# Layer 1 of a two-layer graph attention kernel: gathers without a limit of five in flight, issued by half block

## The chip, the cores and the metric

The kernel runs on one core of a Trainium2 chip. The core has a matrix engine (TensorE, "PE" in the profile; its weight loads are "PEld"), a vector engine (VectorE, "DVE"), a scalar engine (ScalarE, "ACT"), a general engine (GpSimd, "POOL") and a queue engine (SyncE, "SP"), which work side by side and wait for each other on semaphores, and 16 DMA engines that move data between memory and the on-chip SBUF. The metric is the device time of one execution in microseconds. The kernel before has a median of 1829.56 us over three runs (1821.65 to 1831.82).

## The reference

Two graph attention layers over 2708 nodes with 1024 features, in float32. `adj` is a 2708 x 2708 matrix of zeros and ones, symmetric, with ones on the diagonal and about 16 others in a row.

```python
def layer0(x):                       # all products 1024 wide
    f, g = x @ Wf + bf, x @ Wg + bg
    e = relu(f @ g.T)
    attention = softmax(where(adj > 0, e, -9e15), axis=1)
    return attention @ (x @ W + bW)

def layer1(x):
    h = x @ W1
    e = leaky_relu(h @ a1 + (h @ a2).T, 0.2)
    attention = softmax(where(adj > 0, e, -9e15), axis=1)
    return relu(attention @ h)

x = layernorm(x + layer0(x))
x = layernorm(x + layer1(x))
```

## The kernel before

Since a row of `adj` has few ones, the kernel does not compute the 2708 x 2708 scores. A first stage reads `adj`, extracts the neighbours of every node as a list of up to 40, orders the nodes by the length of their lists, and cuts them into 85 groups of 32 nodes. A group whose longest list has up to 4n entries has n *tiles*: `TILES[g]` is 3 to 10. A tile has 128 partitions, four neighbours of each of 32 nodes, and is filled by one *gather*: an indirect DMA issued by POOL (line 180) that fetches 128 rows of a table in memory by the indices in one column of `SL`. Padding in the lists has an index past the table, and such a row is skipped. Four groups form a *block* (the first block is one group alone); there are 22 blocks and 405 tiles.

Layer 0 (lines 855 to 1090) works through the blocks with gathers of `x` into a ring of 20 slots. Its normalised output goes in two places: rows of x1 to the table `X1S`, and rows of x1 with the product by W1 a2 as a further column to the table `T1` (1028 columns, 4112 bytes a row).

Layer 1 (lines 1093 to 1247) is where the change lies. Its ring has 33 slots: the 20 of `ring` and 13 of `more`. Blocks go in order of their number of tiles, and each is cut into two *half blocks* of two groups, 43 in all, with 6 to 14 tiles each (the very first has 3). For half block n, in the order of the program:

- `sums` (line 804): on PE, for each tile four matmuls of its 128 x 512 halves by the weights in `st`, into one of two PSUM halves `po`; afterwards the tiles' slots are put in the set `free`;
- `closing` (line 1203): the scatter of an earlier block's finished rows to `out`, on POOL;
- `lay.gathers()` (line 1206): POOL's gathers for all tiles whose slot (their number less 33) is in `free`;
- a piece of an earlier block's product with W1: 16 matmuls into `pm`, and the transposes `pt` of the half block before;
- `scores1` for half block n + 1 (line 1122): on DVE the scores, the softmax's maximum and the weights `st`, with the exponential on ACT. This reads the last column of each gathered slot, so it waits for the gathers to land; the sums of n + 1 then wait for it;
- `out` on ACT: the sums scaled into `y`;
- `close1` (line 1142): SP loads the block's rows of `X1S` into one of three buffers `rb`, `u1b`, `u2b`; DVE adds them to the product and normalises; the scatter to `out` follows one half block later.

Every engine's instructions are kept in program order (class `InOrder`, line 61). A gather into a used slot must wait for the last reader of that slot: the scores on DVE and the last matmul on PE. The framework also gives each DMA that POOL issues one of eight semaphores in turn, and a DMA waits until the previous one on its semaphore has landed, unless another wait covers that. On top of that, `Halves(..., 5)` at line 1106 sets `flight` to 5: each gather from the sixth on waits for the landing of the fifth gather before it (lines 666 to 672). Layer 0's `Layer` has no `flight`.

Because `lay.gathers()` goes through the slots in order of their number, and each slot has its own last matmul, every gather of a half block carries its own wait for PE. The tiles of a half block are numbered by tile position and then group (line 635), which is also the order in which `sums` reads them.

Of the kernel before, what the change touches and what calls it, by code (L numbers as in the profile page):

```python
# [57 lines left out]
TILES = [SORTED[_g] for _g in GROUPS]  # L58
# [48 lines left out]
def listed_path(ctx, tc, x, adj, Wf, bf, Wg, bg, W, bW, W1, a1, a2, out):  # L107
# [6 lines left out]
    TW = D + 4  # L114
# [18 lines left out]
    pe, dve, act, pool, sp = (InOrder(tc, e) for e in (nc.tensor, nc.vector, nc.scalar, nc.gpsimd, nc.sync))  # L133
# [9 lines left out]
    T1 = dram.tile([N, TW], F32, name="T1")  # L143
# [20 lines left out]
    SL = const.tile([P, NG, QT], I32, name="SL")  # L164
    SL0 = const.tile([P, NSL0, QT], I32, name="SL0")
# [12 lines left out]
        nc.gpsimd.memset(t, 0.0)  # L178

    def gather(engine, dst, table, idx, rows=N):  # L180
        return engine.indirect_dma_start(
            out=dst, out_offset=None, in_=table,
            in_offset=bass.IndirectOffsetOnAxis(ap=idx, axis=0), bounds_check=rows - 1, oob_is_err=False)

# [9 lines left out]
    with tc.tile_pool(name="pre", bufs=1) as pre:  # L194
# [294 lines left out]
        for b in range(NB):  # L489
            n = nsize[b]  # L490
# [15 lines left out]
        t = pre.tile([P, NB], F32, name="badt")  # L506
        nc.vector.scalar_tensor_tensor(t, tot, 1.0, cnt, op0=ALU.mult, op1=ALU.not_equal, accum_out=bad[:, 1:2])
        t = pre.tile([P, NB], F32, name="badu")
        nc.vector.tensor_scalar(t, cnt, 0.0, 0.0, op0=ALU.is_equal, op1=ALU.add, accum_out=bad[:, 2:3])
        t = pre.tile([P, NB], F32, name="badv")  # L510
# [131 lines left out]
    class Layer:  # L642

        def __init__(self, units, rings, width, table, stp, flight=None):
            self.flight, self.issued = flight, []
            self.units, self.table, self.width, self.stp = units, table, width, stp

            self.first = {g: i for i, g in enumerate(g for u in units for g in u.gs)}  # L650
            self.slots = [(t, i) for t in rings for i in range(t.shape[1])]
            self.count = len(self.slots)
            self.order = [(u, g, t) for u in units for _, g, t in u.tiles]
            assert all(self.first[g] < NSL0 for _, g, _ in self.order[:self.count])
            self.next, self.free, self.most = 0, set(), len(self.order)
# [2 lines left out]
            t, k = self.slots[m % self.count]  # L658
            return t[:, k, :self.width]

        def gathers(self):
            while self.next < min(self.most, len(self.order)) and (self.next < self.count or self.next - self.count in self.free):
                u, g, t = self.order[self.next]
                idx = SL[:, g, t:t + 1] if self.next >= self.count else SL0[:, self.first[g], t:t + 1]
                made = gather(pool, self.rows(self.next), self.table, idx)
                if self.flight is not None:
                    if len(self.issued) >= self.flight:
                        tc.add_manual_dep(
                            made.ins, self.issued[-self.flight],
                            mybir.DependencyInfo(mybir.DependencyClass.Sync, mybir.DependencyReason.DATA),  # L670
                            reason="gathers in flight")
                    self.issued.append(made.ins.name)
                self.next += 1

        def soft(self, u):

            sc, shape = u.sc, [P, u.G, u.T]
            mq = small.tile([P, Q], F32, name="mq")
            dve.tensor_reduce(mq[:, :u.G], sc, AX.X, ALU.max)

            m4 = small.tile([32, Q, Q], F32, name="m4")
            for q in range(Q):
                dve.tensor_copy(m4[:, :u.G, q], mq[32 * q:32 * q + 32, :u.G])
            m1 = small.tile([32, Q], F32, name="m1")
            dve.tensor_reduce(m1[:, :u.G], m4[:, :u.G, :], AX.X, ALU.max)
            for q in range(Q):
                dve.tensor_copy(mq[32 * q:32 * q + 32, :u.G], m1[:, :u.G])
            dve.tensor_tensor(sc, sc, mq[:, :u.G].unsqueeze(2).to_broadcast(shape), op=ALU.subtract)
            act.activation(sc, sc, AF.Exp)
            u.st = self.stp.tile([P, MOST, 32], F32, name="st")  # L690
            k = 0
            while k < u.G:

                n, t = 1, TILES[u.gs[k]]
                while k + n < u.G and TILES[u.gs[k + n]] == t:
                    n += 1
                c, some = u.col[k, 0], [P, n, t, 32]
                dve.tensor_tensor(u.st[:, c:c + n * t, :].rearrange("p (g t) i -> p g t i", g=n),
                                  sc[:, k:k + n, :t].unsqueeze(3).to_broadcast(some),
                                  stack.unsqueeze(1).unsqueeze(1).to_broadcast(some), op=ALU.mult)  # L700
                k += n
            u.rs = small.tile([P, Q], F32, name="rs")
            dve.tensor_reduce(u.rs[:, :u.G], sc, AX.X, ALU.add)
# [57 lines left out]
    class Halves(Layer):  # L761
# [42 lines left out]
        def sums(self, u, po, ks):  # L804

            st, at, col = u.st[ks[0]], 0, {}
            for k in ks:
                col[k] = at
                at += TILES[u.gs[k]]
            index = {(k, t): m for m, (k, g, t) in enumerate(u.tiles)}  # L810
            for t in range(max(TILES[u.gs[k]] for k in ks)):
                for k in ks:
                    n = TILES[u.gs[k]]
                    if t < n:
                        for h in range(H):
                            j = place(k, h)
                            pe.matmul(po[j:j + 32], st[:, col[k] + t, :],
                                      self.rows(u.at + index[k, t])[:, h * 512:(h + 1) * 512],
                                      start=(t == 0), stop=(t == n - 1))
            self.free.update(u.at + m for (k, t), m in index.items() if k in ks)  # L820

        def spans(self, ks):

            return [slice(0, P)] if len(ks) == 2 else [slice(place(ks[0], h), place(ks[0], h) + 32) for h in range(H)]
# [19 lines left out]
    def load_lists(b):  # L844
        for g in groups[b]:
            gather(pool, SL[:, g, :], LD[:, :], idq[:, g:g + 1], N * Q)
# [8 lines left out]
    ring = ctx.enter_context(tc.tile_pool(name="ring", bufs=1)).tile([P, R0, TW], F32, name="ring")  # L855
    with ExitStack() as s0s:
# [3 lines left out]
        stp, xp, yp, jp = (new_pool(n, 1) for n in ("stp0", "xp", "yp", "jp0"))  # L860
        zs = new_pool("zp", 1).tile([P, TW], F32, name="z")
        seq = [1, 0, *range(2, NB)]
        units = cut(R0, 2, seq)
        lay = Layer(units, [ring], D, x, stp)
# [147 lines left out]
        for k, u in enumerate(units):  # L1012
# [6 lines left out]
            po = ps_s.tile([P, H, 512], F32, name="po")  # L1019
# [73 lines left out]
    with ExitStack() as s1s:  # L1093
# [3 lines left out]
        stp = new_pool("stp1", 3)  # L1097

        x1 = [rb, u1b, u2b]
        more = new_pool("ring1", 1).tile([P, R1 - R0, TW], F32, name="more")  # L1100

        order1 = sorted(range(NB), key=lambda b: (sum(TILES[g] for g in groups[b]), b))
        units = cut(R1, 2, order1)
        for u in units:
            u.st, u.ri = {}, {}
        lay = Halves(units, [ring, more], TW, T1[:, :], stp, 5)
        done1 = {b: i for i, b in enumerate(order1)}
        for u in units:
            g, at = u.gs[0], lay.first[u.gs[0]]
# [82 lines left out]
        def turn_half(u, ks, y):  # L1192
            b = u.b
            if ks[0] == 0:
                yT[b] = tp.tile([P, KC, P], F32, name="yT")
            steps = lay.turn(y, ks, yT[b])
            next(steps)
            return steps

        for n, (u, ks) in enumerate(parts):  # L1200
            b, po = u.b, banks[:, n % 2, :]
            lay.sums(u, po, ks)
            for _ in closing:
                pass
            closing = iter(())
            lay.gathers()
            made = pieces.pop(0)() if pieces else None
            steps = iter(())
            if turning is not None:
                v, kv, _ = turning  # L1210
                steps = turn_half(*turning)
                if kv[-1] + 1 == v.G:
                    pm = []
                    pieces += [lambda c=v.b, h=h, pm=pm: piece(c, h, pm) for h in range(H)]
            if n + 1 < len(parts):
                scores1(*parts[n + 1])
            y = yp.tile([P, 512], F32, name="y1")
            lay.out(u, po, ks, y)
            for _ in steps:
                pass  # L1220
            turning = u, ks, y
            if ks[-1] + 1 == u.G:
                k = done1[b]
                for i in (2 * k, 2 * k + 1):
                    if i < NB:
                        mark_over(i)
                if k == NB // 2 + 1:
                    count_over()
                if k + 2 == NB:
                    unfit = nc.values_load(flag[0:1, 0:1])  # L1230
            if made is not None:
                closing = close1(*made)
                next(closing)
        while pieces:
            made = pieces.pop(0)()
# [375 lines left out]
```

## Time and profile before

| | |
|---|---|
| median of 3 runs | 1829.56 us (1821.65 to 1831.82) |
| the profiled execution | 1827.94 us, its span 1826.2 us |
| PE busy | 1605.9 us (88%) |
| DVE busy | 1294.1 us (71%) |
| POOL busy | 1184.2 us (65%) |
| ACT busy | 642.9 us (35%) |
| layer 1's gathers | 405 issues, first at 1158.3 us, last at 1767.6 us, about 0.99 us of POOL each |
| sums of layer 1 on PE | 1170 to 1782 us; PE busy 526.75 us in 612.20 |
| POOL's DMA queue, whole span | 132032 packets, 428.29 MB |

The span runs from the first to the last instruction. The page divides it into 40 slices of 45.65 us and gives for each the busy tenths of every engine, the granted PE clock, the mean busy share of the 16 DMA engines and the rate in GB/s. POOL's busy time for a gather is the time to write its descriptors; the data lands later, and the trace gives the time from issue to landing. A wait for several semaphores is put down by the profile to the one that came last by its own reckoning, which can name an engine that had long been done.

### The profile page before, as it was taken

The page shows a single profiled execution, that of the slowest core. Times are in us where ns is not written, and L with a number is a line of the kernel's source. Part 1 is how long each engine was busy: PE and PEld are TensorE (multiplying, and loading weights), DVE is VectorE, ACT ScalarE, POOL GpSimd, SP SyncE. Part 2 cuts the span into 40 slices and gives each one's busy share as a digit, 9 for nine tenths or more (in the row PEclk, how much of TensorE's full clock was granted, in tenths as well). Part 3 has the DMA queues.
Part 4 walks back from the last instruction along what each step waited for, and adds up shares of the span by engine and source line. Part 5 has one row for each costly group of instructions (what it writes and reads, how often), then busy time and mean ns, then how long its engine had stood idle before and what let it go on. Part 6 is the DMA issues. An engine that isn't in the chain of part 4 may idle for free. (4 is left out here: it accounts for less than half of the span.)

```text
span 1826.2 us, 23203 instructions
## 1 busy us (share of the span) xinstructions
PE 1605.9 (88%) x6969; PEld 675.9 (37%) x6969; DVE 1294.1 (71%) x4262; ACT 642.9 (35%) x902; POOL 1184.2 (65%) x1192
## 2 busy tenths in 40 slices
PE   5999489899999999999999999298889798978896
PEld 3444233344444444444444444033333333333332
DVE  5779757888888888888888877365555446545552
ACT  4545344445555555444445552011111111111111
POOL 7888475676666666666666552576777676666650
PEclk8999799999999999999999999699899988989888
DMA  7646167667777777777766774799999999999970
GB/s 276 246 151 234 40 232 303 250 218 260 266 282 284 284 272 280 288 291 283 286 249 237 280 300 178 268 365 321 339 354 364 337 353 330 350 356 350 356 265 37
DMA packets 149987, 502.81 MB, mean 275 GB/s; under 512 B 32340, under 2 KB 32372, under 8 KB 147144
## 3 DMA queue, kind: packets, MB, share of 16 engines
q0 software_dynamic: 132032, 428.29, 64.9%
q1 hardware_dynamic: 10202, 55.72, 8.1%
q10 hardware_dynamic: 7618, 17.23, 2.5%
q8 instruction: 57, 0.93, 0.2%
q14 instruction: 78, 0.64, 0.1%
HBM read 509.64 MB, written 33.75 MB: 298 GB/s over the span
## 5 line engine op out<-in xcount | busy, mean ns | idle before, releaser
L71 POOL DMA_INDIRECT ring<-in_x_dram,SL x405 | 437.1, 1079 | 252.8 <-issue 91.1
L71 DVE SCALAR_TENSOR_TENSOR j<-ring,Fr 128x1024 bf16<-128x1024 f32 x402 | 494.5, 1230 | 81.7 <-DMA ring<-in_x_dram,SL 54.2
L71 PE MATMUL po<-ring,st 128*32 128x512 f32 x2616 | 334.2, 635 | 57.3 <-ACT y L71 40.3
L71 ACT COPY Fr<-pm 32x1024 f32<-32x1024 f32 (+2 forms) x353 | 340.5, 964 | 19.4 <-PE pm L71 14.7
L71 POOL DMA_INDIRECT ring<-T,SL x249 | 246.9, 992 | 114.2 <-issue 43.4
L71 PE MATMUL pm<-M,yT 128*128 128x512 f32 (+1 forms) x704 | 313.3, 598 | 0.5 <-ACT yT L71 0.5
L71 PE MATMUL pm<-M,xT 128*128 128x512 f32 x672 | 304.6, 607 | 0.0
L71 PE MATMUL pm<-Wt,xT 128*128 128x512 f32 (+1 forms) x704 | 303.5, 599 | 1.0 <-DMA Wt<-in_L_gnn_W_dram 1.0
L71 ACT ACTIVATE scores<-scores 128x12 f32<-128x12 f32 (+9 forms) x65 | 14.0, 216 | 726.7 <-DVE scores L71 726.7
L71 POOL DMA_INDIRECT more<-T,SL x156 | 154.6, 991 | 71.3 <-issue 32.8
L71 PEld LDWEIGHTS pm<-M,yT 128*128 128x128 f32 (+1 forms) x704 | 127.9, 186 | 184.6 <-issue 183.1
L71 PEld LDWEIGHTS po<-ring,st 128*32 128x32 f32 x2616 | 103.4, 117 | 243.6 <-issue 192.3
L71 PEld LDWEIGHTS pm<-M,xT 128*128 128x128 f32 x672 | 126.2, 193 | 162.2 <-issue 162.2
L71 PEld LDWEIGHTS pm<-Wt,xT 128*128 128x128 f32 (+1 forms) x704 | 125.1, 186 | 152.8 <-issue 151.0
L409 POOL TENSOR_TENSOR adj<-adj,iota 128x2708 f32<-128x2708 f32 (+3 forms) x23 | 130.5, 5684 | 23.9 <-ACT adj L71 23.8
L71 PE MATMUL po<-more,st 128*32 128x512 f32 x624 | 96.5, 714 | 38.1 <-ACT y L71 38.1
L412 DVE MAX8 cand<-adj 128x8 f32<-128x136 f32 (+2 forms) x440 | 97.3, 285 | 38.3 <-POOL adj L409 38.3
L71 PE MATMUL pm<-halfT,WfT 128*128 128x512 f32 x256 | 114.5, 603 | 1.1 <-ACT WfT L71 1.1
L71 DVE TENSOR_SCALAR scores<-ring,f1q 128x4 f32<-128x4 f32 (+6 forms) x69 | 17.4, 263 | 131.8 <-DMA ring<-T,SL 122.5
L71 POOL DMA_INDIRECT SL<-LD,idq x85 | 85.9, 1011 | 25.8 <-issue 21.2
L71 DVE TENSOR_SCALAR scores<-more,f1q 128x3 f32<-128x3 f32 (+6 forms) x48 | 12.5, 268 | 82.6 <-DMA more<-T,SL 73.7
L71 PEld LDWEIGHTS pm<-halfT,WfT 128*128 128x128 f32 x256 | 48.4, 193 | 58.1 <-issue 55.4
(211 smaller groups left out, 1547.8 us busy)
## 6 DMA issues: line engine op xcount, KB each, us to landing
adj<-in_adj_dram SPq DMA_DIRECT2D x21, 1354.0 KB, 5.9
X1S<-z SPq DMA_DIRECT2D x19, 512.0 KB, 6.5
ring<-in_x_dram,SL POOLq DMA_INDIRECT x405, 6.3
rows<-in_L_gnn_Wg_dram ACTq DMA_DIRECT2D x8, 512.0 KB, 4.4
rows<-in_L_gnn_Wf_dram ACTq DMA_DIRECT2D x8, 512.0 KB, 3.6
rows<-in_L_gnn_W_dram ACTq DMA_DIRECT2D x8, 512.0 KB, 6.3
Wt<-in_L_gnn_W_dram ACTq DMA_DIRECT2D x1, 4096.0 KB
M<-in_L_gnn_W_dram SPq DMA_DIRECT2D x1, 4096.0 KB
```

The source lines that it names most:

```text
L71: made = self.tc.keep_in_program_order(op(*args, **kwargs))
L409: nc.gpsimd.tensor_tensor(k[:n, cut], k[:n, cut], iota[:n, cut], op=ALU.mult)
L412: nc.vector.max(cand[:n, s, :], k[:n, s * SEG:min((s + 1) * SEG, N)])
```

## The change

The argument 5 and the code of the limit are removed. `sums` now returns the number of the tile that it reads last (the last tile of the half block's longest group), and `gathers` first collects all tiles whose slot is free and, if the tile that goes into that last-read slot is among them, issues it ahead of the others. Since that gather waits for the last matmul of the half block, the gathers behind it in POOL's order find their own matmuls done and carry no wait for PE. PE, DVE, ACT and SP have the same instructions in the same order in both kernels; on POOL the same number of gathers, with one of them moved to the front of nearly every batch. In the compiled program each of POOL's DMAs in layer 1 now waits for the eighth of POOL's DMAs before it, through the eight semaphores.

```diff
     def gather(engine, dst, table, idx, rows=N):
-        return engine.indirect_dma_start(
+        engine.indirect_dma_start(
...
-        def __init__(self, units, rings, width, table, stp, flight=None):
-            self.flight, self.issued = flight, []
+        def __init__(self, units, rings, width, table, stp):
...
-        def gathers(self):
+        def gathers(self, latest=None):
+            ready = []
             while self.next < min(self.most, len(self.order)) and (self.next < self.count or self.next - self.count in self.free):
-                u, g, t = self.order[self.next]
-                idx = SL[:, g, t:t + 1] if self.next >= self.count else SL0[:, self.first[g], t:t + 1]
-                made = gather(pool, self.rows(self.next), self.table, idx)
-                if self.flight is not None:
-                    if len(self.issued) >= self.flight:
-                        tc.add_manual_dep(
-                            made.ins, self.issued[-self.flight],
-                            mybir.DependencyInfo(mybir.DependencyClass.Sync, mybir.DependencyReason.DATA),
-                            reason="gathers in flight")
-                    self.issued.append(made.ins.name)
+                ready.append(self.next)
                 self.next += 1
+            if latest is not None and latest + self.count in ready:
+                ready.remove(latest + self.count)
+                ready.insert(0, latest + self.count)
+            for m in ready:
+                u, g, t = self.order[m]
+                idx = SL[:, g, t:t + 1] if m >= self.count else SL0[:, self.first[g], t:t + 1]
+                gather(pool, self.rows(m), self.table, idx)
...
             self.free.update(u.at + m for (k, t), m in index.items() if k in ks)
+            n, k = max((TILES[u.gs[k]], k) for k in ks)
+            return u.at + index[k, n - 1]
...
-        lay = Halves(units, [ring, more], TW, T1[:, :], stp, 5)
+        lay = Halves(units, [ring, more], TW, T1[:, :], stp)
...
-            lay.sums(u, po, ks)
+            latest = lay.sums(u, po, ks)
             for _ in closing:
                 pass
             closing = iter(())
-            lay.gathers()
+            lay.gathers(latest)
```

## The prediction, made before the changed kernel ran

> **What bounds the kernel now.** I read the page first (shares and slices), then stretches of layer 1, POOL's waits, its timeline, and two counts up to one moment. Layer 1 fills the span from its first gather at 1158.3 us to 1826.2; the change touches only the gathers, of which the last starts at 1767.6.
>
> ```profile
> span 1826.2 us, 23203 instructions
> ...
> DMA  7646167667777777777766774799999999999970
> GB/s 276 246 151 234 40 232 303 250 218 260 266 282 284 284 272 280 288 291 283 286 249 237 280 300 178 268 365 321 339 354 364 337 353 330 350 356 350 356 265 37
> ```
>
> From slice 26 the DMA digit stands at 9, yet the rate stays at 321 to 365 GB/s. The stretches (columns: engines' busy us, PE clock, DMA share, GB/s) show why that is not the ceiling:
>
> ```profile
> 1168.00:1178.00 10.00, 5.02 (x12) 1.06 (x12) 3.15 (x22) 0.20 (x1) 7.39 (x8) 0.67 1.02 411
> ...
> 1506.00:1511.00 5.00, 5.00 (x36) 1.65 (x34) 4.51 (x16) 0.64 (x2) 2.40 (x3) 1.00 1.02 411
> 1511.00:1514.00 3.00, 3.00 (x9) 1.33 (x8) 0.56 (x4) 1.24 (x1) 2.05 (x3) 1.00 0.68 256
> 1514.00:1518.00 4.00, 3.02 (x11) 1.30 (x9) 2.18 (x13) 0.00 (x0) 2.35 (x3) 1.00 0.74 202
> ```
>
> 411 GB/s is reached twice, then falls to 256 and 202 within a few microseconds, with the work for those transfers long known. The second dip has POOL's gap just ahead of it:
>
> ```profile
> 1506.81 0.99 POOL L71 DMA_INDIRECT ring<-T,SL  x1 [0.30 <-issue]
> 1510.09 0.99 POOL L71 DMA_INDIRECT ring<-T,SL  x1 [2.29 <-PE po L71]
> 1511.39 0.99 POOL L71 DMA_INDIRECT ring<-T,SL  x1 [0.30 <-issue]
> 1512.68 0.99 POOL L71 DMA_INDIRECT ring<-T,SL  x1 [0.30 <-issue]
> 1515.04 0.99 POOL L71 DMA_INDIRECT ring<-T,SL  x1 [1.37 <-DMA ring<-T,SL]
> ```
>
> Undisturbed, POOL starts a gather every 1.295 us (0.99 of work, 0.30 between). Here 3.28 and 2.36 pass. The releaser "PE po" would mean a slot that is not free yet. The counts from 1158 to 1434.4 us, the end of one half block's sums, refute that:
>
> ```profile
> L71 POOL DMA_INDIRECT ring<-T,SL x120 | 119.1, 993 | 53.1 <-issue 21.0 <-DMA ring<-T,SL 12.6 <-PE po L71 8.6
> L71 POOL DMA_INDIRECT more<-T,SL x67 | 66.4, 990 | 27.4 <-issue 11.5 <-PE po L71 6.5 <-DMA more<-T,SL 3.4
> ...
> L71 PE MATMUL po<-ring,st 128*32 128x512 f32 x448 | 70.1, 697 | 37.7 <-ACT y L71 21.0 <-DVE rs L71 16.7
> L71 PE MATMUL po<-more,st 128*32 128x512 f32 x260 | 37.6, 671 | 14.9 <-ACT y L71 14.9
> ```
>
> 448 + 260 = 708 matmuls at 4 per gathered tile are 177 tiles summed. With 33 slots, gathers up to number 210 could be out; 120 + 67 = 187 are. So POOL is 23 gathers behind what the slots allow, and what holds it is the other wait of each gather: the landing of the fifth before it. Over the whole layer the DVE waits for gathers to land (126.0 us for ring, 83.6 for more), so the gather stream sets the pace: POOL's starts, with the limit of five, and the DMA engines behind them.
>
> ```profile
> DMA to landing us min/median/max: 4.2/6.1/8.7
> ```
>
> This is ring's. Five starts take 5 x 1.295 = 6.5 us, so a median gather just escapes the limit and a slow one, up to 8.7 us, holds POOL.
>
> **The change, part by part.** (1) *The wait on the fifth gather before goes.* The stream runs from 1158.3 to 1767.6, 609.3 us, and holds 405 gathers and 18 scatters to out, so 422 intervals; at 1.295 they are 546.5. The excess is 62.8 us, of which the 88 memsets of "over" take 5.0, so 57 to 58 could go: the upper end of the gain, POOL back to back. What is late next is not "no limit": the compiled order gives each POOL transfer one of eight semaphores in turn, so in the changed kernel each waits for the eighth transfer before it. Eight starts are 10.4 us, above the 8.7 of the slowest landing now; that limit rests unless landings grow by 1.7 us.
>
> The other end is the DMA engines' own time. A full gather is 128 x 4112 bytes = 526 KB, at 411 GB/s 1.281 us; 405 are 518.6. In the stretch also lie 18 scatters and 18 loads of X1S, 524 KB and 1.276 us each: 45.9. Sum 564.5, so 45 us gained if the engines never wait (many rows are skipped as padding, but a transfer is done only when its fullest engine is). The first 33 gathers, which find free slots and no scatter, took 42.4 us for 32 intervals, 1.326 each, 2.4% over 1.295: an estimate of what remains as loss even there. 564.5 x 1.024 = 578, a gain of 31. I take 38, midway between 31 and 45, because the DMA account is the nearest to the stretches shown, and keep 31 and 57 as ends of a full removal.
>
> One row speaks against 38: the nine stretches of 60 us from 1200 to 1740 average 346 GB/s, and the best of them, 1380 to 1440, has 358. Were that the ceiling, only 609 x (1 - 346/358) = 20 us could go. I keep 38, since 411 GB/s was held over 10 us at 1168 and over 5 at 1506. The Trainium skill, page "DMA: Bandwidth & Descriptors", section "Bandwidth", gives about 358 GB/s per core as what HBM lets through to SBUF; by that rule the sum would be the 20. The trace disagrees with it, by the same 411.
>
> (2) *One wait on PE per half block, at its last matmul, and that gather first.* A batch now starts only when the sums end, 3.6 us (32 matmuls) to 7 us (48) after the first slot is free. I cost it at nothing: POOL is 23 gathers (30 us) behind at that moment, so every such wait is long over. If the cover went, each of the 43 half blocks could lose up to 3.6 to 7 us less the 10 us in flight, so nothing much either. PE, whose sums it rests on, must follow: it is busy 526.75 of the 612.2 us from 1170 to 1782.2, leaving 85 idle, more than 38 or 57. Only from 1200 to 1260 is it full (60.00 of 60); there the 6 us that POOL gains become lead, spent in the larger blocks later.
>
> (3) *The order.* One gather of a later tile goes ahead of some eight; a half block that ends inside the batch gets its last tile 1.3 us later, the next one has one early. The stream's length is the same, and the last batch is not reordered (the tile 33 after its last slot does not exist). Zero, 1.3 us at most.
>
> (4) *What is queued behind POOL.* The scatters of out keep their place and now wait for the eighth transfer before them, too. On SP, the load of X1S into the same buffer waits for that scatter's landing: scatter at 1407.63, load at 1414.10, first use by DVE at 1474.98. Some 55 us of cover (32 at the last block: 1772.3 against 1804.5); deeper queues add at most 3 x 1.3 us. Zero. After 1767.6 nothing changes: 58.6 us to the end of the span.
>
> Sum: the profiled execution took 1827.94 us (span 1826.2 and 1.7 around it), 1.6 under the median 1829.56 of runs from 1821.65 to 1831.82. 1829.56 - 38 = 1791.6; I say 1791.
>
> **Rivals.** *Partial gain:* the stragglers stay. The dips come from one late engine (a landing of 8.7 us), and with eight out it still holds the rest now and then; half the stall stays: 10 to 29 us gained, 1800 to 1819. For: the DMA share is already 0.94 from 1170 to 1782. Against: 411 GB/s twice, with five out.
>
> *The memory side is full:* 358 GB/s is the most over any longer time; 20 us gained, 1809. For: no stretch of 60 us has more. Against: the 10 us at 411. This is the skill's rule above as a case of its own.
>
> *POOL back to back:* 57 gained, 1772. For: in layer 0, which has no limit of five, POOL starts ten gathers from 599.93 to 611.58 at 1.294 each, without a gap, at 364 GB/s (600 to 613). Against: the 564.5 us of the DMA engines.
>
> *Nothing moves:* the fullest engine is busy throughout and the waits only show it. 1829, within 9. For: POOL's stalls follow slow landings. Against: a share of 0.68 to 0.74 from 1511 to 1518 means engines standing idle.
>
> *Slower, deeper queues stretch each packet:* from 1685 to 1716 a share of 0.97 moves 354 GB/s, 365 per unit; at 1168 it is 403, 10% more. If the cause of that is contention among transfers and it doubles, 328 x 1.0 against 354 makes the stream 8% longer: +48, 1878; half of it 1853. Even with the share at 1.0 it decides as soon as a unit of it moves under 354, 3% below 365. Against: the low rates stand where few are in flight (202 GB/s at 0.74, 273 per unit, after POOL's gaps), the high ones where five are.
>
> **How the numbers follow.** About half a per cent, 9 us, can be told from no change. Chances: 30 to 50 gained (forecast) 0.45; back to back 0.10; partial 0.11; memory side full 0.05; nothing 0.14; slower 0.15. The partial and memory cases lie nearly all over 9 us: faster 0.70, same 0.15, slower 0.15. The likeliest case alone spans 1780 to 1800. The range from 1770 (full 57 and a little) to 1832 leaves out the slower case and little else.
>
> **What would show it.** POOL's starts in layer 1 mostly 1.295 apart, the last gather near 1730 instead of 1767.6; landings longer, 7 to 10 us at the median, since more are out; DMA share near 1.0 and 380 GB/s or more from 1320 to the end of the stream; PE idle under 60 us. Wrong would be: the last gather still after 1755 with gaps of 2 us before it (the eighth transfer is the limit), landings of 10 us with the same GB/s (the engines were full), or POOL waiting for PE with fewer than 8 gathers of backlog (batching matters after all).

## The result

| | before | after |
|---|---|---|
| median, us | 1830.68 (1821.65 to 1831.82, 4 runs) | 1779.02 (1769.24 to 1780.17, 4 runs) |
| profiled execution, its span | 1827.94, 1826.2 | 1778.06, 1776.3 |
| first and last gather of layer 1 | 1158.3, 1767.6 | 1159.7, 1715.4 |
| GB/s and DMA share, 1200 to 1700 us | 346, 0.95 | 380, 1.00 |

The ratio of the times is 0.9723, with a 95% interval of 0.9696 to 0.975: some 51 us faster. Here and below, ratios and intervals leave out executions that fell in a slower state, while medians keep them: one of four in e1_no_limit and e3_limit6, three of four in e4_limit4, one of ten in e2_order_only, one of the 13 of the kernel before beside these four, and a single execution of 6585.68 us in e12_ring22_slots. The stream of gathers shrank from 609.3 to 555.7 us, by 53.6. It begins 1.4 us later, and the tail behind the last gather is 60.9 us instead of 58.6, so 49.9 us of it arrive in the span.

The page of the changed kernel first (span, DMA share in tenths and rate in 40 slices of 44.4 us).

```profile
span 1776.3 us, 22882 instructions
...
DMA  7646168568777777777787787299999999999960
GB/s 284 245 160 240 44 227 318 207 213 289 291 283 270 264 250 256 272 282 266 277 295 278 268 296 297 88 359 368 365 369 394 392 392 378 383 395 391 391 250 37
```

The last two thirds of the stream run at 378 to 395 GB/s, where before had 330 to 364. The digit of the DMA share is 9 in both kernels. The stretches of the changed kernel (same columns as before: PE, PEld, DVE, ACT and POOL busy, PE clock, DMA share, GB/s):

```profile
1159.00:1716.00 557.00, 488.36 (x2342) 202.89 (x2346) 328.71 (x1570) 80.93 (x184) 424.32 (x511) 0.95 0.99 380
1172.00:1732.30 560.30, 504.62 (x2431) 209.29 (x2431) 335.63 (x1597) 82.17 (x187) 416.18 (x503) 0.96 0.98 374
1506.00:1511.00 5.00, 5.00 (x19) 2.17 (x12) 0.69 (x5) 0.69 (x1) 3.96 (x4) 1.00 1.02 407
1511.00:1514.00 3.00, 3.00 (x15) 1.35 (x17) 0.39 (x1) 0.00 (x0) 2.13 (x3) 1.00 1.04 372
1514.00:1518.00 4.00, 4.00 (x34) 1.18 (x34) 3.69 (x11) 0.65 (x2) 3.08 (x4) 1.00 0.95 338
```

The rate no longer falls to 256 and 202 within a few microseconds of 411. PE, over its sums, is busy 504.62 of 560.30 us: idle 55.7, where before had 85. POOL's timeline in the stretch where before showed gaps of 2.29 and 1.37 us:

```profile
1507.38 0.99 POOL L71 DMA_INDIRECT more<-T,SL  x1 [0.30 <-issue]
1508.67 0.99 POOL L71 DMA_INDIRECT more<-T,SL  x1 [0.30 <-DMA more<-T,SL]
1509.96 0.99 POOL L71 DMA_INDIRECT more<-T,SL  x1 [0.30 <-issue]
1511.26 0.99 POOL L71 DMA_INDIRECT more<-T,SL  x1 [0.30 <-issue]
```

Every start is 1.295 us after the one before. Counted over the whole stream, 401 of the 422 intervals between starts are under 1.35 us (329 in the kernel before) and 2 are over 2 us (33). The longer of the two follows a scatter to `out`:

```profile
1690.83 1.00 POOL L71 DMA_INDIRECT out_dram<-u2b,ids  x1 [0.81 <-DMA ring<-T,SL]
1694.66 1.01 POOL L71 DMA_INDIRECT ring<-T,SL  x1 [2.83 <-issue]
```

What POOL waits for there the profile does not say; the run without the limit alone, below, has the same 2.83 us behind the same scatter. So holds like this are left, but few. The groups of POOL over the stream (1159 to 1716), with the idle time ahead of each and what ended most of it:

```profile
L71 POOL DMA_INDIRECT ring<-T,SL x249 | 246.9, 992 | 83.3 <-issue 69.9 <-DMA T<-ring,ids 5.3 <-DMA ring<-T,SL 3.2
L71 POOL DMA_INDIRECT more<-T,SL x156 | 154.7, 992 | 47.5 <-issue 40.7 <-DMA more<-T,SL 3.5 <-DVE newton L71 0.6
...
L71 POOL MEMSET over<- 128x6 f32 (+6 forms) x88 | 5.0, 127 | 0.2
```

The 405 gathers had 185.5 us of idle time ahead of them in the kernel before (114.2 for ring, 71.3 for more); 130.8 are left, and 405 times the 0.30 us that always lie between two starts are 121.5 of it. The landings of ring's gathers, from issue (the trace has the landing of 33 of the 249; in the kernel before of 63):

```profile
DMA to landing us min/median/max: 5.8/7.1/10.5
```

One microsecond more at the median than before (6.1); the slowest just reaches the 10.4 us of eight starts (among more's it is 10.7). And the counts up to 1403.7 us, the end of the sums of a half block:

```profile
L71 POOL DMA_INDIRECT ring<-T,SL x113 | 112.1, 992 | 38.9 <-issue 30.0 <-DMA T<-ring,ids 5.3 <-DVE scores L71 1.2
L71 POOL DMA_INDIRECT more<-T,SL x66 | 65.4, 992 | 19.5 <-issue 16.8 <-DVE scores L71 0.6 <-DMA more<-T,SL 0.6
L71 PE MATMUL po<-ring,st 128*32 128x512 f32 x400 | 61.2, 683 | 33.4 <-DVE rs L71 17.1 <-ACT y L71 16.3
L71 PE MATMUL po<-more,st 128*32 128x512 f32 x260 | 33.0, 602 | 6.7 <-ACT y L71 6.7
```

660 matmuls are 165 tiles summed, so up to 198 gathers could be out; 179 are. POOL, without the limit of five, is still 19 gathers behind what the slots allow.

### The profile page after: what moved, and what is told of

Its sections match the earlier page's. It is cut to its first block, busy times and chain, and to the rows that moved or that the text cites. A ratio compares the mean times of both kernels' runs of the same rounds, so it can differ in the third digit from the quotient of the medians.

```text
span 1776.3 us, 22882 instructions
## 1 busy us (share of the span) xinstructions
PE 1586.4 (89%) x6969; PEld 677.2 (38%) x6969; DVE 1295.3 (73%) x4262; ACT 643.4 (36%) x902; POOL 1188.0 (67%) x1192
## 5 line engine op out<-in xcount | busy, mean ns | idle before, releaser
L71 DVE SCALAR_TENSOR_TENSOR j<-ring,Fr 128x1024 bf16<-128x1024 f32 x402 | 494.4, 1230 | 82.5 <-DMA ring<-in_x_dram,SL 55.7
L71 PE MATMUL po<-ring,st 128*32 128x512 f32 x2616 | 322.7, 618 | 47.8 <-ACT y L71 30.4
L71 PE MATMUL po<-more,st 128*32 128x512 f32 x624 | 83.8, 632 | 17.8 <-ACT y L71 17.8
L71 ACT ACTIVATE y<-po,ri 128x512 f32<-128x512 f32 (+1 forms) x88 | 57.5, 678 | 20.9 <-PE po L71 20.3
```

The lines of the kernel that those rows point to most:

```text
L71: made = self.tc.keep_in_program_order(op(*args, **kwargs))
```

## The experiments

**The theory** after the result: removing the limit of five is the whole gain, and POOL, which cannot start a gather more often than every 1.295 us, is the bound now. **The rivals**: the handing back of slots in one piece brought part of the gain; the DMA engines are the bound now; the limit of eight semaphores is.

### Which part of the change brings the gain

The limit alone, in the kernel before (its gathers stay in the order of the slots, each with its own wait for PE):

```diff
-        lay = Halves(units, [ring, more], TW, T1[:, :], stp, 5)
+        lay = Halves(units, [ring, more], TW, T1[:, :], stp)
```

> The limit of five removed, gathers in the order of their slots with a wait for PE each, as before. Theory (the limit alone held POOL; slots are about 20 gathers ahead): as the changed kernel, 1779 us within 4, the last gather of layer 1 near 1716 us of the span. Rival (the waits for PE, one per gather, cost POOL part of the 62.8 us of gaps; the profile puts 38.8 us down to them): 20 to 39 us slower than the changed kernel, about 1800 to 1818, with gaps of 0.5 to 2.8 us ahead of gathers put down to PE.

The order alone: the changed kernel, with the limit of five put back into `gathers` and into the call:

```diff
-        lay = Halves(units, [ring, more], TW, T1[:, :], stp)
+        lay = Halves(units, [ring, more], TW, T1[:, :], stp, 5)
```

> The limit of five kept, the new order and the one wait for PE per half block. Theory: as before, 1830 us within 4, POOL's gaps in layer 1 again some 55 to 63 us. Rival (the per-slot waits cost): 20 to 39 us faster than before, 1791 to 1810.

And the limit at 6 and at 4, in the kernel before (`stp, 6` and `stp, 4` in the same line):

> A limit of six in place of five, all else as before. Theory (a gather is held when a landing takes longer than the limit's number of starts at 1.295 us: 7.8 us for six, 6.5 for five; landings before were 6.1 at the median, 8.7 at most): most of the gain, 35 to 45 of the 51 us, so 1786 to 1796. Rival (the DMA engines were always short of work and depth helps in proportion): a third of the way from five to eight, 17 us, 1813.

> A limit of four. Theory: four starts are 5.2 us and the median landing is 6.1, so nearly every gather is held: a gather per (landing + 0.3)/4, and with landings of 5.5 us at a shorter queue 1.45 to 1.6 us each, a stream of 640 to 680 us in place of 609: 1860 to 1900. Rival (the limit only shows full DMA engines): within 10 us of before.

These four ran on a chip on which the kernel before itself took 1940.61 us. There the order alone took 1936.66, a ratio of 0.9964 (0.9923 to 1.0005): nothing, as the theory had it. But no limit took 1976.8, a ratio of 1.0115 (1.0038 to 1.0192), slower than before, and a limit of 6 took 1979.39, 1.0196 (1.0121 to 1.027). A limit of 4 gave a median of 1976.93, but its four executions run from 1937.05 to 1988.98 us, so it cannot be told from the kernel before. The theory had expected the gain of the limit here as well. The waits of PE, ACT and POOL in the no-limit run, from its first gather at 1224 to its last at 1904 (engine and what waits, what ended it: us in total, times, longest), show other work being late:

```profile
PE pm L71 <- issue: 43.0, 55, 1.5
```

```profile
ACT y L71 <- remote: 212.0, 17, 21.6
```

```profile
POOL out_dram L71 <- ACT rb L71: 34.8, 6, 9.1
```

"issue" is time in which PE waited for nothing that the profile shows, and "remote" an end that it puts down to no instruction of this core. POOL's starts took 133 us more than 422 times 1.295 while 310 GB/s were moved, and 96 us of POOL's idle time lie ahead of scatters to `out` and are put down to ACT and DVE (the largest of these groups is shown). So the gathers were not the only thing that was waited for. Why PE and ACT are late on that chip, and why fewer waits make the kernel slower there, stays open. The four are inconclusive for the limit. For the same reason the 0.9964 of the order says little by itself: on that chip the limit's removal brought no gain either. No limit and the limit of 6 were run again on two other chips, where the kernel before takes 1824.11 and 1827.13 us.

> The limit removed alone, again, since the first time the kernel before itself took 1940 us. Theory: where the kernel before takes about 1830 us, this is 0.97 of it, as the changed kernel (1779), with the last gather of layer 1 near 1716 us. Rival (the one wait per half block and the order are part of the gain): 0.98 to 0.99.

No limit alone took 1773.52 us, a ratio of 0.9712 (0.9675 to 0.9749). The changed kernel has 0.9723 (0.9696 to 0.975). Its stream takes 555.1 us (1157.5 to 1712.6), against 555.7. The limit alone is the whole gain, and beside it the order and the single wait for PE add nothing that these intervals can tell.

```profile
1200.00:1700.00 500.00, 458.05 (x2217) 190.66 (x2217) 303.09 (x1435) 75.56 (x171) 382.21 (x468) 0.98 1.00 381
```

The line is that of the changed kernel (380 GB/s, 0.98, 1.00) but for a digit.

> A limit of six in place of five, all else as before; again, since the first time the kernel before took 1940 us. Theory (a gather is held when its landing takes longer than the limit's starts; the kernel without a limit shows landings of 6.7 us at the median and 8.1 at the ninth tenth, six starts are 7.8 us): most of the gain, 35 to 45 us under the kernel before. Rival (depth helps in proportion): 17 us.

A limit of 6 took 1795.17 us, 0.9823 (0.976 to 0.9885): 32 us of gain (21 to 44 by the interval), a little under the theory's range and above the rival's 17. Its stream takes 573.4 us. Its stretch:

```profile
1162.00:1736.00 574.00, 500.57 (x2346) 203.24 (x2350) 326.92 (x1572) 80.99 (x184) 423.88 (x511) 0.93 0.98 368
```

One gather more in flight brings 346 to 368 GB/s, and two more (the eight semaphores) 380. The excess over 422 intervals of 1.295 us goes 62.8, 26.9, 8.6. Landings with six in flight have medians of 6.2 and 6.5 us, under the 7.8 us of six starts, but reach 8.9, so a slow one still holds POOL.

### What bounds the stream now

To load the DMA engines more: the padding, whose rows are skipped, is fetched too, by clipping the list at the last row of the table. The gathers then move full tiles. The list needs room, so the ring has a slot fewer.

```diff
-    R0, R1 = 20, 33
+    R0, R1 = 20, 32
...
+                if self.width == TW:
+                    idx = self.lists[:, g, t:t + 1]
...
+        lay.lists = ovp.tile([P, NG, QT], I32, name="SLF")
+        dve.tensor_scalar(lay.lists, SL, float(N - 1), None, op0=ALU.min)
```

> The changed kernel with layer 1's indices clipped, so that padding fetches a row of the table instead of being skipped (the scores mask it, so nothing else changes), and a ring of 32 slots for 33 to make room for the clipped lists. It measures the account of the DMA engines by itself: every gather moves 128 rows. Theory (that account, 1.281 us per gather and 1.276 per scatter and X1S load, 564.5 us for the stream, was too high for the real kernel because skipped rows shorten the fullest engine too): the stream grows from 555.7 to between 564.5 and 578 us, the time by 9 to 22 us to 1788 to 1801, and POOL shows gaps of some 10 to 25 us again. Rival (POOL's 1.295 us per start hides the engines either way): within 4 us of the changed kernel.

It took 1792.49 us, 0.982 (0.9774 to 0.9865), 19 us over the limit-only kernel on the same chip, where the theory had 9 to 22. The stream takes 571.2 us.

```profile
1200.00:1700.00 500.00, 445.07 (x2119) 178.69 (x2117) 293.82 (x1397) 72.79 (x164) 370.89 (x457) 0.96 1.02 406
```

406 GB/s over 500 us: what the prediction had from 10 us at 411 is a rate that the core holds. It is well above the 358 that the Trainium skill (page "DMA: Bandwidth & Descriptors", section "Bandwidth") names as the limit on the HBM side. The same section gives that figure as the share of each core when both cores of an HBM domain stream, and has 425 GB/s for a core by itself; 406 on the one core that runs this kernel lies between the two. The stream's excess over 422 intervals of 1.295 us is 24.7 us again, and part of it is POOL waiting for landings (the largest such group over the stream; 0.30 of each wait lies between any two starts):

```profile
POOL ring L71 <- DMA ring<-T,SLF: 14.0, 35, 1.2
```

and the median landing is 9.6 us. The bytes can be worked out: 402 GB/s over the 571 us of the stream are 229.5 MB; less 18.9 MB for 18 scatters and 18 loads, over 405 gathers, 520 KB each, near the 526 of a full tile. In the changed kernel 380 GB/s over 557 us are 211.7 MB, less 18.9, over 405: 476 KB. A tenth of the bytes of a tile is skipped, and with them the engines' time: in the traces a skipped row is a packet of 4 bytes that takes 9 ns, a fetched one 4112 bytes and 160 ns at the median. That all the padding reads one and the same row does not show as a cost of its own: a packet of 4112 bytes takes 165 ns in the mean here and 171 in the changed kernel.

To load the DMA engines less: each gather of layer 1 moves half a row (the table seen as 5416 rows of 514), and the sums read that half twice. What is left out is told in the expectation.

```diff
-                gather(pool, self.rows(m), self.table, idx)
+                if self.width == TW:
+                    gather(pool, self.rows(m)[:, TW // 2:], T1.rearrange("n (a d) -> (n a) d", a=2), idx)
+                else:
+                    gather(pool, self.rows(m), self.table, idx)
...
-                                      self.rows(u.at + index[k, t])[:, h * 512:(h + 1) * 512],
+                                      self.rows(u.at + index[k, t])[:, 514:1026],
```

> The changed kernel with each gather of layer 1 moving half a row (2056 of 4112 bytes, 257 KB for 526) with the same number of rows and issues; the sums use that half twice. The result of layer 1 is therefore not the reference's. Theory (POOL's starts alone set the stream now): with half the bytes it still takes 422 starts of 1.295 us, 546.5, and a few us: 548 to 553 for 555, and the time 1768 to 1775 where the kernel before takes 1825 to 1830, 0.967 to 0.972. Rival (the DMA engines set it, share 0.99 to 1.00): the stream shrinks by 60 us or more until PE or POOL binds, but POOL's starts fall under 1.295 us with smaller rows, and the time goes under 1750.

It took 1767.15 us, 0.966 (0.9617 to 0.9703). The stream takes 555.2 us, as with whole rows, 2 us over the theory's 548 to 553; what the run gains lies ahead of it (first gather at 1154.0 against 1157.5 and 1159.7) and behind it (56.4 us of tail against 59 to 61). Its stretch and a piece of POOL's timeline:

```profile
1200.00:1700.00 500.00, 459.48 (x2192) 191.87 (x2188) 302.77 (x1429) 75.12 (x168) 385.00 (x468) 0.97 0.72 210
```

```profile
1503.14 1.00 POOL L71 DMA_INDIRECT more<-T,SL  x1 [0.30 <-DMA more<-T,SL]
1504.45 1.00 POOL L71 DMA_INDIRECT more<-T,SL  x1 [0.30 <-issue]
```

The share of the DMA engines falls to 0.72, landings to a median of 3.8 us, and the starts stay 1.30 apart. That shows POOL's starts to be the bound of the changed kernel. The slowest landing that the trace has is 6.4 us, far under the 10.4 us of eight starts, so the eight semaphores are not the bound either. The run with full tiles shows that the DMA engines follow right behind: a tenth more bytes makes the stream 15.6 us longer.

To load POOL more: a memset of one column behind each gather of layer 1, in the changed kernel.

```diff
+    pad1 = const.tile([P, 1], F32, name="pad1")
...
+                if self.width == TW:
+                    pool.memset(pad1, 0.0)
```

> The changed kernel with one memset of 128 x 1 on POOL after each gather of layer 1, 405 in all. Theory (POOL's own starts now bound the stream): each costs what it takes on POOL, 0.06 to 0.2 us by the memsets of the profile, so 24 to 80 us on the whole. Rival (the DMA engines bound it, with the share at 0.99): POOL has slack, under 10 us.

It took 1777.83 us, 0.9735 (0.9698 to 0.9773): 4 us over the limit-only kernel, where the theory wanted 24 or more. The timeline says why:

```profile
1604.58 0.99 POOL L71 DMA_INDIRECT more<-T,SL  x1 [0.19 <-issue]
1605.56 0.12 POOL L71 MEMSET pad<- 128x1 f32 x1
1605.87 0.99 POOL L71 DMA_INDIRECT more<-T,SL  x1 [0.19 <-issue]
```

The memset takes 0.12 us out of the 0.30 between two gathers, and the starts stay 1.29 apart. So this run, though it came out as the rival has it (under 10 us), told nothing of the bound: it added next to no load.

To load POOL less: the marks of the valid entries (`over`, 88 memsets on POOL in the stream) go to DVE.

```diff
-                        pool.memset(over[32 * q:32 * q + valid[0], 0, TILES[0]:], 1.0)
+                        dve.memset(over[32 * q:32 * q + valid[0], 0, TILES[0]:], 1.0)
...
-                    pool.memset(over[:, g, TILES[g]:], 1.0)
+                    dve.memset(over[:, g, TILES[g]:], 1.0)
...
-        pool.memset(over, 0.0)
+        dve.memset(over, 0.0)
```

> The changed kernel with the 88 memsets of over, and the one ahead of them, moved from POOL to DVE. Theory (POOL bound): their 5.0 us and some of the 0.9 us ahead of each next gather leave the stream: 4 to 9 us faster, 1770 to 1775. Rival (the DMA engines bound it): no change within 3 us, or slower by what DVE's scores are put off.

It took 1773.75 us, 0.9713 (0.9676 to 0.975), and its stream 552.5 us. The stream is 2.6 us shorter than with no limit alone, but it begins 3.1 us later and the tail is 1.4 longer, so the time is the same (1773.52): the theory's 4 to 9 us are not there. In the changed kernel the 88 marks lie in 12 of the 422 intervals, and these take 3.8 us more than 12 times 1.295, so no more than that could go. By its time alone the run fits the rival (no change within 3 us) as well; what tells the two apart is the run with half rows.

### When the handing back in one piece matters

The prediction costed the batch at nothing because POOL is 19 or more gathers behind the slots. To take that cover away, the ring has 22 slots instead of 33, once in the changed kernel and once in the kernel without a limit that keeps the order of the slots and a wait for each:

```diff
-    R0, R1 = 20, 33
+    R0, R1 = 20, 22
```

> The changed kernel with a ring of 22 slots for 33, so that slots are short: at the start of a half block's sums the kernel with 33 had 8 to 16 free slots not yet used, mostly 12 to 14, so with 22 it has none to 5. Theory: POOL now waits for the sums, and the batch that starts only at their end costs up to 3.6 to 7 us per half block, less what the eight in flight cover: slower than the same ring with a wait per slot by 20 to 100 us; both slower than with 33. Rival (batching costs nothing at any ring, since the eight in flight cover it): the two rings of 22 within 5 us of each other.

> The kernel without the limit, gathers in the order of their slots with a wait for PE each, and a ring of 22 slots. Theory: as under the ring of 22 with batches, 20 to 100 us faster than that one, still slower than with 33 slots by 10 us or more. Rival: within 5 us of the batches.

The batch took 1839.64 us, 1.0064 (1.0043 to 1.0086), 0.6% slower than before. A wait for each slot took 1802.97, 0.9837 (0.9781 to 0.9894). With 22 slots the batch costs 36.7 us. The streams take 625.6 and 583.2 us. POOL's timeline of the batch:

```profile
1501.58 0.99 POOL L71 DMA_INDIRECT ring<-T,SL  x1 [0.31 <-issue]
1506.35 0.99 POOL L71 DMA_INDIRECT ring<-T,SL  x1 [3.78 <-PE po L71]
```

and PE's:

```profile
1498.42 7.65 PE L71 MATMUL po<-ring,st 128*32 128x512 f32 x48 [4.55 <-ACT y L71]
```

48 matmuls run from 1498.42 to about 1506.1, and the gather that goes into the slot read last starts 0.3 us after. The slots of the tiles before it have been free for up to 7 us. The waits of POOL for PE over the stream, first of the batch, then with a wait for each slot:

```profile
POOL ring L71 <- PE po L71: 38.0, 9, 7.7
```

```profile
POOL ring L71 <- PE po L71: 18.8, 64, 0.3
```

Nine waits of up to 7.7 us against 64 of no more than the 0.3 between two starts. With one of 3.5 us ahead of a gather into `more` the batch's waits for PE are 41.5 us.

## Why the prediction was right, and where it was off

The time, 1779.02, lies in the range, a microsecond beyond the quick end of the likeliest case (1780 to 1800): the gain is 51 us where 38 was forecast. That the forecast came within 12 us owes something to luck, since the DMA engines' account that it was taken from is not what bounds the changed kernel; the range held because its other end was POOL back to back.

- **The bound before and the mechanism** were right. POOL was held by the landing of the fifth gather before, not by slots; no limit alone gives the whole gain (0.9712), which leaves nothing to the order.
- **The size** was off: the mis-sized term of the sum is the DMA engines' account, 564.5 us, or 578 with its loss. The prediction took the value between gains of 31 and 45 "because the DMA account is the nearest to the stretches shown". The stream took 555.7, and the other end was the right one: POOL back to back, 546.5 us and 9.2 over it, of which the marks have 3.8. The account was made with 526 KB a gather; skipped rows leave 476. The prediction did see the padding, and set it aside since a transfer ends with its fullest engine. The run with full tiles gives 571.2 us, between the account's two ends: the account is right for the tiles that it was made for, and wrong for these. That transfers in flight behind a padded one used the engines that its padding left idle is argued from this and from the 9 ns of a skipped row; no view shows it engine by engine. The rows of before held the number: 346 GB/s over 609.3 us are 210.8 MB, less 18.9, over 405, 474 KB; at 411 GB/s 1.153 us each, 513 us with the scatters and loads, under POOL's 546.5. So POOL was the higher of the two limits from the start, and the rival "POOL back to back" (57 gained, 1772) was the better forecast.
- **The eight semaphores** hold next to nothing, as said, though the margin is gone: landings grew by 1 us at the median and to 10.7 at most, against 10.4. Two gaps over 2 us are left. Six in flight (573.4 us) instead of eight would have cost 18.
- **The batch and the order** cost nothing, and for the reason given: 19 gathers of cover at 1403.7 us. Their price without the cover was too low: the prediction had "nothing much either"; with 22 slots it measured 36.7 us. It subtracted the 10 us in flight from the wait, but while POOL waits nothing is started, and up to 7.7 us at a time come back as an idle POOL, in ten waits over the stream.
- **PE** could follow: idle 55.7 us (forecast under 60). **What is behind POOL** had its cover: the tail grew by 2.3 us.
- **The signs**: starts 1.295 apart, yes; last gather 1715.4, not near 1730; landings 7.1, at the lower end; share 0.99; 378 to 395 GB/s from slice 30 on.
- **The rivals**: the memory side is not full at 358 (380 in the change, 406 with full tiles); the forecast was right to set this figure aside. Deeper queues did not stretch packets: 380 GB/s at a share of 0.99 are 384 for a unit of share, against 365 (354 at 0.97). Nothing like the half stall of the partial gain is left.

## What to carry to other kernels

A limit on gathers in flight should be over the slowest landing divided by the spacing of the starts: 8.7 / 1.295 is 6.7, so five stalls, six stalls a little, and eight hardly does. Landings grow with the depth (10.7 at most with eight, 8.3 starts), so the division has to be done again at the new depth; seven was not run. Before a transfer limit is set against an engine's issue limit, take the bytes from rate times time in the trace and not from the tile, when rows can be skipped. And handing buffers back in one piece is free only while the consumer of the free buffers is further behind than the piece is long; with shorter rings it took 36.7 us.

## What the runs showed of the hardware that was not expected

- The spacing of two gathers' starts on POOL is 1.295 us with rows of 4112 bytes and 1.30 with rows of 2056. A memset of 0.12 us in the 0.30 us between them costs next to nothing: 405 of them, 4 us.
- One core held 406 GB/s for 500 us with gathers of full rows. A row that a gather skips is still a packet, of 4 bytes and 9 ns.
- On one chip the kernel before took 1940.61 us, with PE and ACT late for reasons that the profile does not name, and there the same edit that gained 2.9% elsewhere lost 1.1%.
